# Long-convolution taps of a Macaron layer: products over 64 x 16 positions in place of 128 x 8

## The chip, the cores and the metric

The kernel runs on one core of a Trainium2 chip. The metric is the device time of one execution in microseconds (us). A core has TensorE (PE in the profile; PEld is its weight load), VectorE (DVE), ScalarE (ACT), GpSimd (POOL) and SyncE (SP, which here only issues DMAs).[...]

## The reference

A Macaron layer over x (4 sequences of 1024 positions, 256 channels): half a feed-forward layer, a long convolution along the sequence, half a feed-forward layer again, each on a layer norm and added to x. Cut to what matters:

```python
x = x + 0.5 * ffn(layernorm(x))
x = x + attn(layernorm(x))
x = x + 0.5 * ffn(layernorm(x))

# ffn: 256 -> 1024 (two, gated) -> 1024 -> 1024 -> 256
h = silu(tlin(x, w1)) * tlin(x, w2)
h = gelu(tlin(h, h1)); h = gelu(tlin(h, h2))
return tlin(h, w3)

# attn: a diagonal state-space convolution, its kernel K has 1024 taps per channel
dt = exp(log_dt)[:, None]; A = -exp(log_A_real) + 1j * A_imag
C = (C_real + 1j * C_imag) * (exp(A * dt) - 1) / A
K = 2 * einsum('dn,dnl->dl', C, exp((A * dt)[:, :, None] * t)).real   # 32 modes n
y = irfft(rfft(K, 2 * L) * rfft(x, 2 * L))[:L]
return gelu(y) @ W.T + b
```

Everything is float32.

## The kernel before

**Blocks.** The 4096 positions are cut into 8 blocks of 512. The first feed-forward layer runs over blocks f0 to f7, the second over g0 to g7, one after the other, in `ffn` (L247). In a block, the first layer makes `pa` and `pb` (L254, L255), the second and third make `p` (L268), each in 8 columns m of 16 matmuls (`linear`, L239: 8 input tiles, each as a high and a low part), and the output product `po` (L295) ends it. A column is evicted by ScalarE (activation into `g`, copy into `h`, L271 and L273) and VectorE (low part, L217). The next block's input is loaded, normalised and transposed (`pt`, L225) by `prepare` (L774), which advances one step (`ahead`) per column of the third layer.

**Side work.** All that is not feed-forward is one Python generator, `all_aside` (L794): first the taps of the convolution (`kernel_steps`, L446), then their spectrum (`kernel_spectrum`, L610, products `pf_k`), then for each sequence b the convolution itself (`mix`, L638: spectrum of x with products `pf_m`, product with the taps' spectrum, inverse transform with sums on VectorE, products `pi` L731, Gelu into `yt`, products `pw` L751), then comparisons of the weights held with those given (L328). `ffn` calls `tick` 15 times a block: after each column but the last of the second and third layers, and once before the output product. Each tick runs the generator to its next `yield`. So the order on every engine is fixed by where the yields stand.

`mix(b)` waits in the generator until block f(2b+1) is done. The blocks g(2b) and g(2b+1) need its result in HBM (x2), so `prepare` for a g block begins with

```python
            while ("m", blk // 2) not in done:
                next(aside, None)
            xb = load_x(x2, blk, f"x_{name}")
```

which runs all missing steps of the side work at once; `done` gets its entry when the generator is resumed after the last `yield` of `mix`.

**The taps.** Position t of a tap is split as t = NB a + b. For each channel a product over 128 rows (32 modes, real and imaginary, for two halves of the channels) gives all positions: the stationary operand holds the powers at NB a (128 values of a), the moving one, `qd`, those at b times C (8 values of b for each half of the channels, the other half's rows zero). Powers at NB a are an outer product of 16 fine and 8 coarse powers (`to_re`, `to_im`): three VectorE operations for 4 channel pairs (L525 to L527). `powers` (L422) makes a 128 x 512 tile of powers with exp and sin on ScalarE. The channel pairs come in two groups of 64. The four products of a step are issued one tick after their operand (`ready`, `products`); when a PSUM tile `pk` is full (32 pairs), ScalarE copies it to the four `taps` tiles (L508).

`taps` has partition a and, for each b, the channels. In `spectrum` (L538) it is multiplied by cosine and sine matrices (`forward`, loaded by `matrix`, L551), and partition p stands for position 8 p + j.

Working tiles of 2 KB a partition (`half`) share 19 buffers[...].

Of the kernel before, what the change touches and what calls it, by code (L numbers as in the profile page):

```python
# [15 lines left out]
ALU = mybir.AluOpType  # L16

P = 128
B, L, D = 4, 1024, 256
HID = 1024  # L20
J = L // P
DC = D // P
KH = HID // P
TB = 512
JT = TB // P
N2 = 32
DD = D // 2
NB = L // P
A0, A1 = 16, 8
JQ = J // 2  # L30
N_CHECKS = 44

# [15 lines left out]
C_A0, C_A1 = 0, A0  # L48
# [43 lines left out]
def macaron_layers(  # L92
# [37 lines left out]
    def half(name, *shape, dtype=F32):  # L130

        return work.tile([P, *(shape or (512,))], dtype, tag="half", name=name, bufs=19)
# [289 lines left out]
    def powers(d0, first, n, name):  # L422


        ch = 512 // n
        at = cst_sb[:, None, first : first + n].to_broadcast([P, ch, n])

        def of(i):
            return adt[:, i, d0 : d0 + ch, None].to_broadcast([P, ch, n])

        a, k, e = (half(f"{t}_{name}", ch, n) for t in ("a", "k", "e"))
        tt(e, of(0), at, ALU.mult)
        nc.scalar.activation(e, e, AF.Exp)
        tt(a, of(1), at, ALU.mult)
        reduce_angle(a, a, k)
        yield
        c = k
        sin_cos(c, a)
        yield
        tt(c, c, e, ALU.mult)  # L440
        tt(a, a, e, ALU.mult)
        yield c, a
# [2 lines left out]

    def kernel_steps():  # L446

        yield from kernel_factors()
        taps.extend(half(f"taps_{i}", 2, 2, DD) for i in range(NB // 2))
        n = TB // P  # L450
        group = 512 // NB
        shape = [P, n, A1, A0]
        for g0 in range(0, DD, group):

            for got in powers(g0, C_A1, A1, f"1_{g0}"):
                yield
            c, i = got
            to_re, to_im = half(f"to_re_{g0}", group, A1), half(f"to_im_{g0}", group, A1)
            ts(to_re, c, column(C_RE), None, ALU.mult)
            stt(to_re, i, column(C_IM), to_re, ALU.mult, ALU.add)  # L460
            ts(to_im, c, column(C_IM), None, ALU.mult)
            stt(to_im, i, column(C_MINUS_RE), to_im, ALU.mult, ALU.add)
            yield
            fine = []
            for d0 in range(g0, g0 + group, 512 // A0):
                for got in powers(d0, C_A0, A0, f"0_{d0}"):
                    yield
                fine.append(got)

            for got in powers(g0, C_B, NB, f"b_{g0}"):  # L470
                yield
            c, i = got
            for t, m in ((c, 0), (i, 1)):
                tt(t, t, c_dt[:, m, g0 : g0 + group, None].to_broadcast([P, group, NB]), ALU.mult)
            yield
            qd = []
            for d1 in range(0, group, per_tile):
                t = half(f"qd_{g0 + d1}", per_tile, 2, NB)
                nc.gpsimd.memset(t, 0.0)
                qd.append(t)  # L480
                for h in range(2):
                    part, ch = slice(h * 64, (h + 1) * 64), slice(d1, d1 + per_tile)
                    tt(t[part, :, h, :], c[part, ch], i[part, ch], ALU.add)
            yield

            pk = None
            ready = []

            def products():

                nonlocal pk
                for d1, a in ready:
                    at = d1 % per_tile
                    if at == 0:
                        pk = psum.tile([P, per_tile, 2, NB], F32, tag="ps", name=f"pk_{g0 + d1}")
                    for i in range(n):
                        nc.tensor.matmul(  # L497
                            pk[:, at + i, :, :].rearrange("p h b -> p (h b)"),
                            a[:, i].rearrange("p a b -> p (a b)"),
                            qd[d1 // per_tile][:, at + i, :, :].rearrange("p h b -> p (h b)"),  # L500
                            start=True,
                            stop=True,
                        )
                    if at + n == per_tile:
                        first = g0 + d1 + n - per_tile
                        for i, t in enumerate(taps):
                            for h in range(2):
                                nc.scalar.copy(  # L508
                                    t[:, :, h, first : first + per_tile],
                                    pk[:, :, h, 2 * i : 2 * i + 2].rearrange("p d b -> p b d"),  # L510
                                )
                ready.clear()

            for d1 in range(0, group, n):
                re, im = fine[d1 // (512 // A0)]
                at = d1 % (512 // A0)

                def outer(coarse, t):
                    return (
                        coarse[:, d1 : d1 + n, :, None].to_broadcast(shape),  # L520
                        t[:, at : at + n, None, :].to_broadcast(shape),
                    )

                a, o = (half(f"{t}_{g0 + d1}", n, A1, A0) for t in ("p", "po"))
                tt(a, *outer(to_re, re), ALU.mult)  # L525
                tt(o, *outer(to_im, im), ALU.mult)
                tt(a, a, o, ALU.add)  # L527
                products()
                ready.append((d1, a))
                yield  # L530
            products()
            yield

# [1 line left out]
    def swapped(t):  # L535
        return t[:, ::-1, :]

    def spectrum(rows_of, name):  # L538

        def add(a, b, op, tag):
            o = half(f"{tag}_{name}", 2, D)
            tt(o, a, b, op)
            return o

        u, v = {}, {}
        order = (0, 2, 1, 3)
        evicted = {}

        def matrix(q):  # L551
            m = half(f"m_{name}_{q}", 2, 2, P)
            nc.sync.dma_start(m, forward[:, 2 * q : 2 * q + 2])
            return m

        def products(q, m):
            ps = []
            for e in range(2):
                ps.append(psum.tile([P, 2, D], F32, tag="ps", name=f"pf_{name}_{q}_{e}"))
                for part in range(2):  # L560
                    nc.tensor.matmul(  # L561
                        ps[e][:, part, :], m[:, e, part, :], rows_of(q + JQ * e), start=True, stop=True
                    )
            other = half(f"f_{name}_{q}", 2, D)
            nc.scalar.copy(other, ps[1])
            evicted[q] = ps[0], other

        def sums(q):
            p, other = evicted.pop(q)
            u[q] = add(p, other, ALU.add, f"u{q}")  # L570
            v[q] = add(p, other, ALU.subtract, f"v{q}")

        m_next = matrix(order[0])
        yield
        got = {}
        for n, q in enumerate(order):
            m = m_next
            if n + 1 < len(order):
                m_next = matrix(order[n + 1])
            products(q, m)  # L580
            if n:
                sums(order[n - 1])
            if n == 3:
                a0 = add(u[0], u[2], ALU.add, "a0")
                a1 = add(u[0], u[2], ALU.subtract, "a1")
            yield
        sums(order[3])
        b0, b1 = add(u[1], u[3], ALU.add, "b0"), add(u[1], u[3], ALU.subtract, "b1")
        yield
        got[0], got[4] = add(a0, b0, ALU.add, "x0"), add(a0, b0, ALU.subtract, "x4")  # L590
        got[2, 6] = add(a1, swapped(b1), ALU.add, "x26")
        got[6, 2] = add(a1, swapped(b1), ALU.subtract, "x62")
        yield
        c, d = add(v[0], swapped(v[2]), ALU.add, "c"), add(v[0], swapped(v[2]), ALU.subtract, "d")
        e, f = add(v[1], swapped(v[3]), ALU.add, "e"), add(v[1], swapped(v[3]), ALU.subtract, "f")
        yield
        g, h = add(e, swapped(f), ALU.add, "g"), add(e, swapped(f), ALU.subtract, "h")
        for key, r, by, t in (
            ((1, 7), g, SQRT_HALF, c),
            ((5, 3), g, -SQRT_HALF, c),  # L600
            ((3, 5), swapped(h), SQRT_HALF, d),
            ((7, 1), swapped(h), -SQRT_HALF, d),
        ):
            got[key] = half(f"x{key[0]}{key[1]}_{name}", 2, D)
            stt(got[key], r, by, t, ALU.mult, ALU.add)
            if key == (5, 3):
                yield
        yield got

    def kernel_spectrum():  # L610
# [2 lines left out]
            return taps[j // 2][:, j % 2].rearrange("p h d -> p (h d)")  # L613

        got = None
        for got in spectrum(rows_of, "k"):
            yield
        minus = half("k_minus", 2, D)
        for n, m in enumerate((0, 4)):
# [292 lines left out]
```

## Time and profile before

| | |
|---|---|
| median of 3 runs | 1465.45 us (1464.86 to 1466.04) |
| the profiled execution | 1466.05 us, its span 1464.1 us |
| granted TensorE clock | 0.995 |
| PE busy | 1429.7 us, 98% |
| PEld busy | 1213.7 us, 83% |
| DVE busy | 860.5 us, 59% |
| ACT busy | 666.1 us, 45% |
| POOL busy | 74.4 us, 5% |
| tap products `pk` on PE | 256 records, first at 156.8, last at 437.7 us |
| copies `taps` <- `pk` on ACT | 32, 237 ns median |

The span is the time from the first to the last instruction of the profiled execution, about 2 us less than its device time. Busy times overlap. Every float32 matmul of the tap products leaves two records, each with its own weight load. A row of a group reads: line, engine, operation, output <- inputs (for a matmul the moving operand comes first), shapes, count, then busy time, mean ns of one, idle time of the engine just before it and what ended that. In the strip of 40 slices each digit is the busy share of 36.6 us in tenths. A line of waits reads: who waited, for whom, us in total, times, longest. A line of the chain or the timeline reads: start, us, engine, what.

### The profile page before, as it was taken

How to read it: one execution, taken by the hardware profiler on the slowest of the kernel's cores; microseconds unless marked ns; L12 is line 12 of the kernel's file. 1: busy time of each engine (PE TensorE's matmuls, PEld its weight loads, DVE VectorE, ACT ScalarE, POOL GpSimd, SP SyncE). 2: the span in 40 equal slices, each digit the busy share in tenths (PEclk: the TensorE clock that was granted, in tenths of full speed). 3: DMA queues.
4: the chain of work that ended last, by engine and by line, in shares of the span. 5: the costliest groups of instructions: out<-in, count | busy, mean ns of one | idle time of the engine just before them, and what ended most of it. 6: DMA issues, size and time to landing. Idle time of an engine off the chain costs nothing.

```text
span 1464.1 us, 18076 instructions
## 1 busy us (share of the span) xinstructions
PE 1429.7 (98%) x7074; PEld 1213.7 (83%) x7074; DVE 860.5 (59%) x1616; ACT 666.1 (45%) x996; POOL 74.4 (5%) x71
## 2 busy tenths in 40 slices
PE   5999999999999999997999999999999999999997
PEld 4788888888888888886888888888888888888886
DVE  5776574765744634667367673676736667464521
ACT  3677353783534434442454344543445334353432
POOL 2000000000000000000100001000010000100000
PEclk9999999999999999999999999999999999999999
DMA  9110000100001111210312113121121111633000
GB/s 365 33 42 2 15 30 4 40 1 29 15 29 44 62 46 38 72 58 29 101 51 87 37 36 94 48 89 37 36 94 44 65 37 36 221 117 101 21 9 17
DMA packets 42975, 85.50 MB, mean 58 GB/s; under 512 B 4737, under 2 KB 9985, under 8 KB 42881
## 3 DMA queue, kind: packets, MB, share of 16 engines
q1 hardware_dynamic: 39088, 72.73, 15.1%
q0 software_dynamic: 3792, 11.54, 2.2%
q8 instruction: 57, 0.93, 0.3%
q14 instruction: 38, 0.30, 0.1%
HBM read 69.05 MB, written 15.20 MB: 58 GB/s over the span
## 4 chain that ended last, share of the span: by engine, by line
PE 94%; DMA 2%; DVE 2%; ACT 1%; issue 0%; POOL 0%; SPq 0%; POOLq 0%; DVEq 0%
PE p_f L239 32%; PE p_g L239 30%; PE po_f L295 4%; PE po_g L295 4%; PE pa_g L239 4%; PE pb_g L239 4%; PE pa_f L239 3%; PE pb_f L239 3%; PE pi L731 2%; PE pf_m L561 2%; PE pk L497 2%; PE pw L751 2%; DMA x_f<-in_x_dram 1%; DMA k_in<-in_kin_dram 1%; PE pt_f L225 1%; DVE given L328 1%
## 5 line engine op out<-in xcount | busy, mean ns | idle before, releaser
L239 PE MATMUL p_f<-ha_f,h_sb 128*128 128x512 f32 x1024 | 242.4, 394 | 1.8 <-ACT ha_f L261 0.9
L239 PE MATMUL p_f<-h_f,h_sb 128*128 128x512 f32 x1024 | 240.4, 392 | 0.0
L239 PE MATMUL p_g<-h_g,h_sb 128*128 128x512 f32 x1024 | 236.0, 390 | 0.0
L239 PE MATMUL p_g<-ha_g,h_sb 128*128 128x512 f32 x1024 | 234.5, 390 | 0.0
L239 PEld LDWEIGHTS p_f<-ha_f,h_sb 128*128 128x128 f32 x1024 | 192.2, 189 | 43.5 <-ACT ha_f L261 1.6
L239 PEld LDWEIGHTS p_g<-ha_g,h_sb 128*128 128x128 f32 x1024 | 192.2, 188 | 39.9
L239 PEld LDWEIGHTS p_g<-h_g,h_sb 128*128 128x128 f32 x1024 | 192.2, 188 | 39.8
L239 PEld LDWEIGHTS p_f<-h_f,h_sb 128*128 128x128 f32 x1024 | 190.9, 188 | 40.0 <-DVE h_f L217 0.3
L271 ACT ACTIVATE g_g<-p_g,sc_sb 128x512 f32<-128x512 f32 x128 | 88.2, 689 | 273.4 <-PE p_g L239 268.6
L217 DVE TENSOR_TENSOR h_f<-g_f,h_f 128x512 fp32r<-128x512 f32 x128 | 88.3, 691 | 193.0 <-ACT h_f L273 192.8
L271 ACT ACTIVATE g_f<-p_f,sc_sb 128x512 f32<-128x512 f32 x128 | 88.0, 688 | 245.6 <-PE p_f L239 245.3
L217 DVE TENSOR_TENSOR h_g<-g_g,h_g 128x512 fp32r<-128x512 f32 x128 | 88.4, 691 | 171.4 <-ACT h_g L273 171.1
L273 ACT CAST h_g<-g_g 128x512 fp32r<-128x512 f32 x128 | 79.4, 620 | 3.9
L273 ACT CAST h_f<-g_f 128x512 fp32r<-128x512 f32 x128 | 79.1, 619 | 3.4
L258 ACT ACTIVATE g_g<-pa_g,sc_sb 128x512 f32<-128x512 f32 x64 | 44.0, 687 | 66.5 <-PE pa_g L239 64.4
L239 PE MATMUL pa_f<-xt_f,w_sb 128*128 128x512 f32 x256 | 70.5, 395 | 1.8 <-DVE xt_f L229 1.2
L259 DVE SCALAR_TENSOR_TENSOR g_g<-pb_g,sc_sb,g_g 128x512 f32<-128x512 f32 x64 | 47.9, 748 | 37.2 <-PE pb_g L239 29.8
L239 PE MATMUL pb_f<-xt_f,w_sb 128*128 128x512 f32 x256 | 69.2, 392 | 0.0
L239 PE MATMUL pa_g<-xt_g,w_sb 128*128 128x512 f32 x256 | 68.6, 390 | 0.0
L239 PE MATMUL pb_g<-xt_g,w_sb 128*128 128x512 f32 x256 | 68.4, 389 | 0.0
L295 PE MATMUL po_g<-w_sb,h_g 128*128 128x256 f32 x512 | 64.2, 285 | 2.2 <-DVE h_g L217 2.2
L295 PEld LDWEIGHTS po_g<-w_sb,h_g 128*128 128x128 f32 x512 | 62.3, 192 | 2.9 <-DVE h_g L217 2.8
(216 smaller groups left out, 1682.3 us busy)
## 6 DMA issues: line engine op xcount, KB each, us to landing
h_sb<-in_h_dram POOLq DMA_DIRECT2D x8, 1024.0 KB, 22.6
given<-in_h_dram SPq DMA_DIRECT2D x32, 256.0 KB, 4.7
kr<-k_hat SPq DMA_DIRECT2D x20, 256.0 KB, 2.7
ki<-k_hat SPq DMA_DIRECT2D x20, 256.0 KB, 2.9
x_f<-in_x_dram SPq DMA_DIRECT2D x8, 512.0 KB, 3.8
xr_f<-in_x_dram SPq DMA_DIRECT2D x16, 256.0 KB, 3.5
x<-y_f SPq DMA_DIRECT2D x16, 256.0 KB, 2.4
xm<-x SPq DMA_DIRECT2D x8, 512.0 KB, 4.1
```

Of the source, the lines that this page charges most:

```text
L217: tt(t[:, 1, :], src, t[:, 0, :].bitcast(F32), ALU.subtract)
L225: nc.tensor.transpose(pt[:, i * P : (i + 1) * P], xn[:, i, k * P : (k + 1) * P], ident)
L239: nc.tensor.matmul(ps, w[:, k, m * P : (m + 1) * P], acts[k][:, part, :], start=(k == 0 and part == 0), stop=(k == n - 1 and part == parts ...
L258: nc.scalar.activation(g, pa, AF.Silu, scale=sc_sb[:, 0, m : m + 1])
L259: stt(g if split else t[:, 0, :], pb, sc_sb[:, 1, m : m + 1], g, ALU.mult, ALU.mult)
L271: nc.scalar.activation(g, ps, AF.Gelu, scale=sc_sb[:, layer, m : m + 1])
L273: nc.scalar.copy(t[:, 0, :], g)
L295: nc.tensor.matmul(ps[:, e * D : (e + 1) * D], ha[k][:, part, (i + e) * P : (i + e + 1) * P], w3_sb[:, k, :], start=(k == 0 and part == 0) ...
L497: nc.tensor.matmul(pk[:, at + i, :, :].rearrange("p h b -> p (h b)"), a[:, i].rearrange("p a b -> p (a b)"), qd[d1 // per_tile][:, at + i, ...
L561: nc.tensor.matmul(ps[e][:, part, :], m[:, e, part, :], rows_of(q + JQ * e), start=True, stop=True)
L731: nc.tensor.matmul(banks[dc][e][:, q * P : (q + 1) * P], vs[q + JQ * e][:, part, dc * P : (dc + 1) * P], m[:, e, part, :], start=(part == ...
L751: nc.tensor.matmul(ps[:, e * D : (e + 1) * D], yts[dc][j // JQ][:, (j % JQ + e) * P : (j % JQ + e + 1) * P], wt_sb[:, dc, :], start=(dc == 0),
```

## The change

The split becomes t = 16 a + b, with 64 values of a (8 coarse by 8 fine) and 16 of b. A product's stationary operand has 64 columns and its moving one 32. An outer-product step covers 8 channel pairs instead of 4, so there are 16 steps instead of 32. The `b` powers of a group come in two chunks of 32 channel pairs instead of one call for 64, and the fine powers in one call instead of two. A `pk` tile holds 16 pairs, uses partitions 0 to 63, and is copied twice into each `taps` tile: b from 0 to 7 to partitions 0 to 63, b from 8 to 15 to partitions 64 to 127. So partition 64 o + a stands for row 2 a + o of before, and for the taps `matrix` loads the rows of `forward` in that order, in two DMAs.

```diff
--- before.py
+++ after.py
@@ -25,8 +25,9 @@
 JT = TB // P
 N2 = 32
 DD = D // 2
-NB = L // P
-A0, A1 = 16, 8
+
+NA, NB = 64, 16
+A0, A1 = 8, 8
 JQ = J // 2
 N_CHECKS = 44
 
@@ -445,10 +446,11 @@
 
     def kernel_steps():
 
+
         yield from kernel_factors()
-        taps.extend(half(f"taps_{i}", 2, 2, DD) for i in range(NB // 2))
-        n = TB // P
-        group = 512 // NB
+        taps.extend(half(f"taps_{i}", 2, 2, DD) for i in range(J // 2))
+        n = 512 // NA
+        group = 512 // A1
         shape = [P, n, A1, A0]
         for g0 in range(0, DD, group):
 
@@ -461,27 +463,26 @@
             ts(to_im, c, column(C_IM), None, ALU.mult)
             stt(to_im, i, column(C_MINUS_RE), to_im, ALU.mult, ALU.add)
             yield
-            fine = []
-            for d0 in range(g0, g0 + group, 512 // A0):
-                for got in powers(d0, C_A0, A0, f"0_{d0}"):
+            for fine in powers(g0, C_A0, A0, f"0_{g0}"):
+                yield
+
+            qd = []
+            some = 512 // NB
+            for d0 in range(g0, g0 + group, some):
+                for got in powers(d0, C_B, NB, f"b_{d0}"):
                     yield
-                fine.append(got)
-
-            for got in powers(g0, C_B, NB, f"b_{g0}"):
+                c, i = got
+                for t, m in ((c, 0), (i, 1)):
+                    by = c_dt[:, m, d0 : d0 + some, None].to_broadcast([P, some, NB])
+                    tt(t, t, by, ALU.mult)
+                for d1 in range(0, some, per_tile):
+                    t = half(f"qd_{d0 + d1}", per_tile, 2, NB)
+                    nc.gpsimd.memset(t, 0.0)
+                    qd.append(t)
+                    for h in range(2):
+                        part, ch = slice(h * 64, (h + 1) * 64), slice(d1, d1 + per_tile)
+                        tt(t[part, :, h, :], c[part, ch], i[part, ch], ALU.add)
                 yield
-            c, i = got
-            for t, m in ((c, 0), (i, 1)):
-                tt(t, t, c_dt[:, m, g0 : g0 + group, None].to_broadcast([P, group, NB]), ALU.mult)
-            yield
-            qd = []
-            for d1 in range(0, group, per_tile):
-                t = half(f"qd_{g0 + d1}", per_tile, 2, NB)
-                nc.gpsimd.memset(t, 0.0)
-                qd.append(t)
-                for h in range(2):
-                    part, ch = slice(h * 64, (h + 1) * 64), slice(d1, d1 + per_tile)
-                    tt(t[part, :, h, :], c[part, ch], i[part, ch], ALU.add)
-            yield
 
             pk = None
             ready = []
@@ -495,7 +496,7 @@
                         pk = psum.tile([P, per_tile, 2, NB], F32, tag="ps", name=f"pk_{g0 + d1}")
                     for i in range(n):
                         nc.tensor.matmul(
-                            pk[:, at + i, :, :].rearrange("p h b -> p (h b)"),
+                            pk[0:NA, at + i, :, :].rearrange("p h b -> p (h b)"),
                             a[:, i].rearrange("p a b -> p (a b)"),
                             qd[d1 // per_tile][:, at + i, :, :].rearrange("p h b -> p (h b)"),
                             start=True,
@@ -504,21 +505,21 @@
                     if at + n == per_tile:
                         first = g0 + d1 + n - per_tile
                         for i, t in enumerate(taps):
-                            for h in range(2):
+                            for over in range(NB // J):
+                                b0 = over * J + 2 * i
                                 nc.scalar.copy(
-                                    t[:, :, h, first : first + per_tile],
-                                    pk[:, :, h, 2 * i : 2 * i + 2].rearrange("p d b -> p b d"),
+                                    t[over * NA : (over + 1) * NA, :, :, first : first + per_tile],
+                                    pk[0:NA, :, :, b0 : b0 + 2].rearrange("p d h b -> p b h d"),
                                 )
                 ready.clear()
 
             for d1 in range(0, group, n):
-                re, im = fine[d1 // (512 // A0)]
-                at = d1 % (512 // A0)
+                re, im = fine
 
                 def outer(coarse, t):
                     return (
                         coarse[:, d1 : d1 + n, :, None].to_broadcast(shape),
-                        t[:, at : at + n, None, :].to_broadcast(shape),
+                        t[:, d1 : d1 + n, None, :].to_broadcast(shape),
                     )
 
                 a, o = (half(f"{t}_{g0 + d1}", n, A1, A0) for t in ("p", "po"))
@@ -535,7 +536,8 @@
     def swapped(t):
         return t[:, ::-1, :]
 
-    def spectrum(rows_of, name):
+    def spectrum(rows_of, name, over=1):
+
 
 
 
@@ -550,7 +552,11 @@
 
         def matrix(q):
             m = half(f"m_{name}_{q}", 2, 2, P)
-            nc.sync.dma_start(m, forward[:, 2 * q : 2 * q + 2])
+            for o in range(over):
+                nc.sync.dma_start(
+                    m[o * (P // over) : (o + 1) * (P // over)],
+                    forward.rearrange("(a o) j t k -> o a j t k", o=over)[o, :, 2 * q : 2 * q + 2],
+                )
             return m
 
         def products(q, m):
@@ -613,7 +619,7 @@
             return taps[j // 2][:, j % 2].rearrange("p h d -> p (h d)")
 
         got = None
-        for got in spectrum(rows_of, "k"):
+        for got in spectrum(rows_of, "k", over=NB // J):
             yield
         minus = half("k_minus", 2, D)
         for n, m in enumerate((0, 4)):
```

## The prediction

> **What bounds the kernel now.** I read the page first: busy shares, slices, chain by engine.
>
> ```profile
> PE 1429.7 (98%) x7074; PEld 1213.7 (83%) x7074; DVE 860.5 (59%) x1616; ACT 666.1 (45%) x996; POOL 74.4 (5%) x71
> PE   5999999999999999997999999999999999999997
> PE 94%; DMA 2%; DVE 2%; ACT 1%; issue 0%; POOL 0%; SPq 0%; POOLq 0%; DVEq 0%
> ```
>
> TensorE is the bound: 94% of the chain is PE. VectorE and ScalarE have slack, so the VectorE work that the change removes pays nothing by itself. What can pay is (a) time PE spends on the convolution-kernel products, and (b) the one dip inside the run, the "7" in slice 19 (695 to 732 us). The start (slice 0) is loading and is not touched.
>
> For (a), the groups with shapes kept apart, then PE's timeline at 161 us:
>
> ```profile
> L497 PEld LDWEIGHTS pk<-qd,p 128*128 128x128 f32 x256 | 33.3, 191 | 2.3
> L497 PE MATMUL pk<-qd,p 128*128 128x16 f32 x256 | 30.7, 252 | 0.0
> ```
> ```profile
> 161.34 0.96 PE L497 MATMUL pk<-qd,p 128*128 128x16 f32 x8
> 162.14 3.93 PE L239 MATMUL p_f<-h_f,h_sb 128*128 128x512 f32 x16
> 165.91 0.96 PE L497 MATMUL pk<-qd,p 128*128 128x16 f32 x8
> ```
>
> Each of the 128 products leaves two records, hence x256. The column after the operation is the stationary shape, here 128 rows by 128 columns, and the moving tile has 16 columns. A feed-forward column of 16 matmuls takes 3.63 us alone (chain: "480.94 3.63 PE p_f"). With four products behind it the period is 165.91 - 161.34 = 4.57, and over the next ones 4.58. So a step of four costs 0.95 us of PE, 32 steps 30.4 us. The blocks confirm it: from output product to output product f1 takes 186.08 - 98.44 = 87.64; a block without side work takes 80.23 (last block) + 0.79 for its transposes; the rest is 6.6 = seven steps.
>
> For (b), the chain of waits on PE, then the chain that ended last at two places:
>
> ```profile
> PE pt_f L225 <- DVE x_f L211: 13.8, 1, 13.8
> PE pi L731 <- DVE v_False L722: 7.4, 1, 7.4
> PE po_g L295 <- DVE h_g L217: 2.2, 2, 1.3
> ```
> ```profile
> 629.88 7.68 PE po_f L295 x64
> 692.11 9.49 PE pi L731 x64
> 740.03 7.67 PE po_f L295 x64
> 822.88 7.67 PE po_g L295 x64
> 877.73 7.14 PE pi L731 x64
> 923.27 7.67 PE po_g L295 x64
> ```
>
> Apart from the first transposes, PE has one long wait: 7.4 us, once, for VectorE's inverse-transform sums, and those `pi` products then run 9.49 instead of 7.14. Block f7 (629.88 to 740.03) is 110.15 long; block g1, with the same side work (`pi`, `pw`, three `pf_m`), is 100.39. The difference, 9.8, is the stall.
>
> Why only there: each block gives 15 ticks, and preparing g0 needs mixing 0 finished. Its demand, counted in the generators: factors 6, two groups of 32, spectrum 15, mixing 35, one resume: 121. Seven blocks plus the seven ticks of f7's second layer offer 112. The loop in `prepare` forces the missing nine at once, and they contain VectorE's whole tail of mixing 0. Before g2, g4 and g6 five are missing; those begin at `pi`, whose inputs are ready, and PE does not wait.
>
> **What the Trainium skill says.** "TensorE: Matmul & The Clock Gate", section "LDWEIGHTS (loading the stationary operand)": load time goes with the stationary columns, at columns / 1.2 ns, so 107 for 128 and 53 for 64, and not with rows. The trace agrees: `pi`, also 128 columns, spends 7.14 us on 64 records, 112 ns each, and `pk` 0.95/8 = 119 with entry. Better still, the trace has one load with a single column:
>
> ```profile
> L835 PEld LDWEIGHTS p_bad<-ones,total x2: 79/80/82, 1456.4 to 1456.4; 128*1 128x1 f32 x2
> ```
>
> 191 - 80 = 111 ns for 127 columns, 0.87 ns each. The same page, section "Wait — 56ns, not 53.3ns?", gives a floor of about 25 ns from matmul start to start; no row shows a case that meets it. "TensorEngine Tiling (Array Packing)", "Key Properties": changing the tiling mode drains the engine. The trace does not show a return from such a change; `p_bad` has nothing after it.
>
> **The change part by part.**
>
> 1. *Products* (L497). Still 128, so 256 records, but 64 stationary columns and 32 moving ones. Loads set the pace before (two records move 2 x 16 columns in almost nothing), so a record falls from 112 to 64 x 0.87 = 56 ns. Moving 32 columns instead of 16 stays under that (`pi` streams 128 in 112 ns, so 32 in about 28). A step of eight has 16 x 56 = 0.90 us plus an entry of 0.95 - 8 x 0.112 = 0.05: 0.95, and there are 16. New PE time 15.2; I take 15.9 for uneven pacing. **Gain 14.5.** Bounds: 45 ns a record gives 12.3 (gain 18); columns not mattering gives 16 x (16 x 0.112 + 0.05) = 29.5 (gain 0.9). A drain of up to 0.17 us on entry and on exit (from the one-column matmul's 163 ns) would take 32 x 0.17 = 5.4 back.
>
> 2. *Ticks.* A group now yields 4 (coarse) + 3 (fine) + 8 (two `b` chunks) + 9 (outer loop) = 24 times instead of 32: 16 fewer. Demand before g0 falls to 105 of 112 offered: nothing is forced, `pi` of mixing 0 lands in f6's third layer at tick pace. Before g2, 140 of 142: none. Before g4, 175 of 172: three, only `pw`. Before g6, 210 of 205: five, as before, and from there both kernels are in the same place, the weight checks too. **Gain 9.7** (7.37 waiting + 2.35 slow `pi`). Next to be late: in f6 the next block's norm shares VectorE with the sums: 0.7 + 1.7 + 4 x 0.6 = 4.8 us, ready 6.1 after PE's third column, where PE wants them at 3.63 + 2 x 1.78 = 7.2. A margin of about 1 us.
>
> 3. *VectorE*: outer products 96 to 48 (48 x 0.69 = 33 us less); `c_dt` products 4 to 8 (+2.7); `qd` sums 8 to 16 (+3.3); the eight calls of `powers` keep number and size. Net 27 less, behind PE's 98%: nothing.
>
> 4. *ScalarE*: tap copies 32 to 64, half as many partitions, same 64 elements. Eight start within 1.1 us (213.96 to 215.5 with a cast between); every other tick gets such a burst beside 1.3 us of activation and cast, in at least 3.63. Zero; if the move to upper partitions doubled a copy, 2.2 + 1.3 still fits.
>
> 5. *POOL*: memsets of 0.53 us, 4 to 8. POOL is 5% busy. Behind them stand the output additions, which no PE work awaits soon. *SP*: the four `m_k` loads become eight of half size; landing is 3.0 us, the load is issued a tick (3.6) ahead, and a second issue adds 0.33. Behind on SP are the next loads, with blocks of slack. Zero; bounded by 4 x 0.3 if PE waited each time.
>
> 6. *Unseen small waits*: other helpers now fall beside block ends, where PE's last columns leave about half a microsecond of slack. I take 0.7 lost; bounds -1 (one of today's small waits goes) to +3.
>
> Sum: -14.5 - 9.7 + 0.7 = -23.5. The profiled execution (1466.05, span 1464.1) becomes 1442.5, span 1440.6; it lay 0.6 above the median of 1465.45, so the median forecast is **1442.0**.
>
> **Rivals.**
> - *Columns do not set the pace* (the array is filled at full width, or the change of form drains each time so that little remains): products gain 0.9 only, 1465.45 - 10.6 + 0.7 = 1455.5. For it: no load of 64 columns in the trace. Against: the 80 ns load. 0.12.
> - *The stall moves*: the same sums are waited for in f6, or a block end pays; 9.7 comes back in part, say 8: 1450. For: the 1 us margin. Against: five-step forcings cost nothing today. 0.10.
> - *The change of form keeps loads from running ahead*: each record then pays load and matmul in turn, 136 + 163 = about 300 ns, 256 of them 77 us for 30.4; less the 9.7, 1502. It decides against the change from (30.4 + 9.7)/256 = 157 ns a record. For: the drain sentence. Against: both `p_bad` loads start at 1456.4, the second not held by the first matmul. 0.04.
> - *The schedule does not follow the count*, so that the nine forced steps stay: 1451.7. The counted positions match the trace for all blocks before. 0.02.
>
> **How the numbers follow.** The forecast case has the remaining 0.72: 1438.5 (45 ns) to 1447.5 (drains). The range of 8 in 10 runs from 1438.0 to 1452.0: it takes in the moved stall and leaves out the first rival and the slow one. About 0.2% (3 us) is what a measurement here can tell from no change. Only the drain rival is slower; between drain and no drain a record of some 150 ns would give "same".
>
> **What would show it.** Right: `pk` loads near 135 ns (80 + 64 x 0.87), 16 bursts of about 0.95 us, PE without a wait at `pi`, f7 near 100 us instead of 110, VectorE about 27 us less, the last two g blocks unchanged. Wrong: bursts of 1.8 us or more, gaps on PE before or after them, or a PE wait for `v_False` or `h_f` in f6.

## The result and the profile after

The changed kernel takes 1446.8 us (median of 4, 1445.27 to 1448.97) against 1465.65 before (4 runs): a ratio of 0.9874, with a 95% interval of [0.9859, 0.9889], some 18.5 us less. The forecast was 1442.0 with a range of 1438.0 to 1452.0. The profiled execution took 1447.1, its span 1445.3, 18.8 less than the span before.

The page of the changed kernel, busy shares, PE's slices and the chain by engine (the lines of the file have moved by one to six):

```profile
PE 1418.6 (98%) x7074; PEld 1199.6 (83%) x7074; DVE 835.7 (58%) x1580; ACT 672.7 (47%) x1026; POOL 76.1 (5%) x75
PE   5999999999999999999999999999999999999997
PE 93%; DMA 3%; DVE 3%; ACT 1%; issue 0%; POOL 0%; SPq 0%; POOLq 0%; DVEq 0%
```

The "7" in slice 19 is gone and nothing has come in its place. PE is the bound as before. VectorE lost 24.8 us of work; none of PE's waits had been for that work, so by itself this bought nothing.

The waits of PE, longest first, and then the chain from the output product of f5 to that of f6:

```profile
PE pt_f L226 <- DVE x_f L212: 13.6, 1, 13.6
PE po_g L296 <- DVE h_g L218: 1.7, 2, 1.3
```
```profile
538.22 7.67 PE po_f L296 x64
...
607.57 7.14 PE pi L737 x64
...
629.96 3.46 PE pw L757 x16
633.42 7.67 PE po_f L296 x64
```

`pi` of mixing 0 now lies in f6 (from the output product of f5 to that of f6), runs its undisturbed 7.14 us, and PE no longer waits for `v_False`. By PE's timeline, f7 lasts 88.2 us instead of 110.0; f6 has taken over `pi` and `pw` and lasts 95.1 instead of 88.3.

The products themselves, by the tile `pk` and then in the chain. The records of one tick that stand together are called a burst here; a burst and the feed-forward column after it make a step:

```profile
L498 PEld LDWEIGHTS pk<-qd,p x256: 132/138/138, 156.8 to 342.6; 128*64 128x64 f32 x128
```
```profile
161.77 1.05 PE pk L498 x16
162.82 3.85 PE p_f L240 x16
166.67 1.05 PE pk L498 x16
```

A load has 138 ns where the forecast said 135. But a step takes 166.67 - 161.77 = 4.90 us. Less the column alone (3.63) that is 1.27, where the forecast had 0.95: the burst is 1.05 instead of 0.90, and the column after it is 0.22 longer, not 0.05. Sixteen steps cost 20.3 us instead of the 15.2 worked out and the 15.9 taken.

So the account of the span is: products 30.4 to 20.3, -10.1; stall of f7, -9.75 (f7 less g1 in the profile before); about +1 in block g6 (84.8 against 83.8 us). Sum -18.8, as measured. Nothing ties the last term to the change: in the kernels below, with the same work in g6, that block takes anything from 83.2 to 85.4.

One thing has to be known to read the times below: the moment at which f0's output product starts lies between 95.4 and 98.7 us in these profiles, although the tap products begin only after it. Part of that is the granted clock: between 40 and 50 us it was 0.83 to 0.85 in five of the twelve profiles, where that moment is at 97.2 or later, and 1.00 in the other seven, where it is at 97.0 or earlier. Before and after are both among the five. Steps inside a profile are therefore compared, rather than single times. The five kernels below for which no time is given were executed once each (1436.6 to 1453.3 us); only their steps are read.

### The profile page after: what moved, and what is told of

It is laid out like the page before. It is cut to its first block, busy times and chain, and to the rows that moved or that the text cites. A ratio compares the mean times of both kernels' runs of the same rounds, so it can differ in the third digit from the quotient of the medians.

```text
span 1445.3 us, 18115 instructions
## 1 busy us (share of the span) xinstructions
PE 1418.6 (98%) x7074; PEld 1199.6 (83%) x7074; DVE 835.7 (58%) x1580; ACT 672.7 (47%) x1026; POOL 76.1 (5%) x75
## 4 chain that ended last, share of the span: by engine, by line
PE 93%; DMA 3%; DVE 3%; ACT 1%; issue 0%; POOL 0%; SPq 0%; POOLq 0%; DVEq 0%
PE p_f L240 31%; PE p_g L240 30%; PE po_g L296 4%; PE po_f L296 4%; PE pa_g L240 4%; PE pb_g L240 4%; PE pa_f L240 4%; PE pb_f L240 4%; PE pi L737 2%; PE pf_m L567 2%; PE pw L757 2%; PE pk L498 1%; DMA x_f<-in_x_dram 1%; DMA k_in<-in_kin_dram 1%; DMA x_g<-x 1%; PE pt_f L226 1%
## 5 line engine op out<-in xcount | busy, mean ns | idle before, releaser
L272 ACT ACTIVATE g_g<-p_g,sc_sb 128x512 f32<-128x512 f32 x128 | 88.3, 690 | 273.7 <-PE p_g L240 273.6
L218 DVE TENSOR_TENSOR h_f<-g_f,h_f 128x512 fp32r<-128x512 f32 x128 | 88.2, 691 | 202.9 <-ACT h_f L274 202.6
```

The lines of the kernel that those rows point to most:

```text
L218: tt(t[:, 1, :], src, t[:, 0, :].bitcast(F32), ALU.subtract)
L272: nc.scalar.activation(g, ps, AF.Gelu, scale=sc_sb[:, layer, m : m + 1])
```

## The experiments

**Schedule alone.** Theory: half of the gain is the tick count and has nothing to do with 64 by 16. Rival: the stall only moves, or the new form of the products is what counts. The first kernel is that of before, with two outer-product steps to a tick:

```diff
-            for d1 in range(0, group, n):
-                re, im = fine[d1 // (512 // A0)]
+            for d2 in range(0, group, 2 * n):
+                fresh = []
+                for d1 in (d2, d2 + n):
+                    re, im = fine[d1 // (512 // A0)]
...
-                products()
-                ready.append((d1, a))
+                    fresh.append((d1, a))
+                products()
+                ready.extend(fresh)
                 yield
```

> The kernel before with its 128 by 8 products, but two outer-product steps to a tick, so that the side work has the 16 ticks fewer of the change and nothing else of it. Schedule theory: the wait of pi in f7 goes, f7 falls from 110.0 to about 88 us and f6 takes the pi and pw products; products cost 30.4 less 16 exits of 0.15, so the time falls by 9.7 + 2.4 = 12, to about 1453.5. Rival, the stall only moves to f6: the time stays within 3 us of before.

Measured: 1454.85 us, ratio 0.9934 [0.9917, 0.9950], which is 9.7 us, give or take 2.4. PE's waits, longest first:

```profile
PE pt_f L225 <- DVE x_f L211: 14.1, 1, 14.1
PE po_g L295 <- DVE h_g L217: 1.8, 2, 1.3
```

No `pi`; f7 lasts 88.2 us. The time alone could hold the 2.4 us expected on top, but the timeline has no room for them: the two bursts of a tick mostly stand apart, with some 6 or 7 matmuls of the feed-forward column between them, and there are 30 bursts, where the kernel before has 32. The kernel's text issues these two bursts one right after the other. So the yields do not fix the order on PE down to the single matmul, as the description of the kernel before has it; what moved them apart, no run shows.

The second kernel is the changed one with the tick count of before:

```diff
                 ready.append((d1, a))
                 yield
+                yield
```

> The changed kernel with one empty yield more after each of the 16 outer-product steps, so that the tick count of the kernel before is back and the 64 by 16 products stay. Schedule theory: nine steps are forced before g0 again, PE waits 7.4 us for v_False, the time rises by 9.7 to about 1456.5. Rival, the changed form of the products itself brought the time: it stays near 1446.8.

Measured: 1454.34 us, ratio 0.9938 [0.9921, 0.9954]: 0.0064 above the change, or 9.4 us of its gain undone. Each kernel is set against the kernel before as timed beside it. The wait is back, word for word apart from the line numbers:

```profile
PE pi L738 <- DVE v_False L729: 7.4, 1, 7.4
```

The two parts add up: 0.9934 x 0.9938 = 0.9872, against 0.9874 for the change. The tick count brings about 9.7 us and the products about 9.1, each within some 2.4. The stall did not move.

**What a record costs.** A burst is longer than forecast. Three theories: the moving columns add to the load (sum), the load sets the pace (load), or the change between 128 and 64 columns costs something (form). The first kernel loads 128 columns again, with 32 moving:

```diff
-                            pk[0:NA, at + i, :, :].rearrange("p h b -> p (h b)"),
-                            a[:, i].rearrange("p a b -> p (a b)"),
+                            pk[:, at + i, :, :].rearrange("p h b -> p (h b)"),
+                            a[:, i // 2 * 2 : i // 2 * 2 + 2].rearrange("p d a b -> p (d a b)"),
...
```

> The changed kernel, each product with the operand of two channel pairs as 128 stationary columns, 32 moving ones as in the change; the result for a pair is read from the half of the partitions that is its own (128 copies instead of 64). Sum theory, a record costs its load and its moving columns one after the other[...], a burst of sixteen 1.9 us, a step 2.1. Load theory, the load alone sets the pace and moving is hidden: 100 to 112 ns, burst 1.6 to 1.8. Form theory, the 0.22 us on the column after a burst is the change between 64 and 128 columns: here it falls to 0.15 as before.

Its chain:

```profile
160.75 1.71 PE pk L498 x16
162.46 3.75 PE p_f L240 x16
```

The burst takes 1.71, where the sum theory wanted 1.9: 107 ns a record, so 32 moving columns are hidden behind a load of 128. The column after the burst is 0.12 longer, not 0.22, as the form theory said. The whole step takes 1.71 + 3.75 = 5.46, so the products cost 5.46 - 3.63 = 1.83.

The second kernel keeps 64 columns and streams 64:

```diff
-                            pk[0:NA, at + i, :, :].rearrange("p h b -> p (h b)"),
+                            pk[0:NA, at + i // 2 * 2 : at + i // 2 * 2 + 2, :, :].rearrange("p d h b -> p (d h b)"),
...
-                            qd[d1 // per_tile][:, at + i, :, :].rearrange("p h b -> p (h b)"),
+                            qd[d1 // per_tile][:, at + i // 2 * 2 : at + i // 2 * 2 + 2, :, :].rearrange("p d h b -> p (d h b)"),
```

> The changed kernel with 64 stationary columns and 64 moving ones in each product: the columns of the neighbouring pair are streamed too and overwrite its result, so half the taps are wrong ones. Sum theory: [...]burst 1.28 us, step 1.5. Load theory: moving stays hidden, 66 ns, burst 1.05, step 1.27 as in the change. The burst against that of the change (1.05) tells them apart.

```profile
164.01 1.08 PE pk L498 x16
165.09 3.85 PE p_f L240 x16
```

1.08 instead of 1.05, where the sum theory wanted 1.28: it falls. Up to 64 moving columns are nearly free here.

**Slope and offset.** What remains is either a load that is slower than its columns say, or a cost for each burst. Issuing the products of two steps together halves the number of bursts:

```diff
                 tt(a, a, o, ALU.add)
-                products()
+                if d1 // n % 2 == 0:
+                    products()
```

> The changed kernel with the products of two outer-product steps issued in one tick: 8 bursts of 32 records instead of 16 of 16. Burst theory: 66 ns a record and 0.22 us for each burst, so a burst with its end takes 2.32 and all of them 18.6 instead of 20.3 us, time down by 1.8. Record theory, the 0.22 goes with the records: 2.54 a burst, no gain.

```profile
158.10 1.98 PE pk L498 x32
160.08 7.48 PE p_f L240 x32
```

Two columns alone are 7.26 us. So thirty-two records and what follows cost 9.46 - 7.26 = 2.20 us, sixteen cost 1.27. Two points give a line: (2.20 - 1.27)/16 = **58 ns a record and 0.34 us a burst**. The single records agree: inside a burst they start 58 ns apart (median). The 2.20 is better than the 2.32 expected, since 66 ns a record had the entry of a burst in it. The eight bursts cost 17.6 instead of 20.3, and the kernel takes 1443.26 us, ratio 0.9860 [0.9841, 0.9878]: below the change, with an interval that overlaps its. Inside the profiles, from f0's output product to that of g7, this kernel is 2.6 us shorter than the changed one, as the steps say.

The same for 32 columns, in bursts of 16 and 32:

```diff
-                            pk[0:NA, at + i, :, :].rearrange("p h b -> p (h b)"),
-                            a[:, i].rearrange("p a b -> p (a b)"),
+                            pk[0:32, at + i, :, :].rearrange("p h b -> p (h b)"),
+                            a[:, i].rearrange("p a b -> p (a b)")[:, 0:32],
...
```

> The changed kernel with only the first 32 of the 64 stationary columns in each product; the other half of the taps stays zero. Column theory, a record's pace follows its columns: 107 ns at 128 and 66 at 64 go on to about 45 at 32, burst 0.7 us. Floor theory, a record cannot go below some 60 to 66 ns however few columns it loads: burst stays at 1.0 to 1.05 us.

> The changed kernel with the first 32 stationary columns only (the other half of the taps stays zero) and the products of two steps in one tick. With 32 columns a burst of 16 and its end cost 0.84 us. Column theory, 28 ns a record and the rest for each burst: 32 records 1.29 us. Floor theory, a record stands on its own at 50 ns: 32 records 1.66.

Chain with bursts of 16, then with bursts of 32:

```profile
160.11 0.62 PE pk L500 x16
160.73 3.85 PE p_f L240 x16
```
```profile
159.37 1.13 PE pk L500 x32
160.50 7.48 PE p_f L240 x32
167.97 1.13 PE pk L500 x32
```

0.84 and 8.60 - 7.26 = 1.34 us: 31 ns a record and again 0.34 a burst. The floor theory falls.

**Which loads pay for a burst.** At full width the line through 8 records (0.95, before, with 16 moving columns) and 16 (1.83, with 32) is 110 ns and 0.07 us. So the narrow products pay 0.27 more for each burst. Is it the form, or any load below full width? 96 columns tell:

```diff
-                            pk[0:NA, at + i, :, :].rearrange("p h b -> p (h b)"),
-                            a[:, i].rearrange("p a b -> p (a b)"),
+                            pk[0:96, at + i, :, :].rearrange("p h b -> p (h b)"),
+                            a[:, i // 2 * 2 : i // 2 * 2 + 2].rearrange("p d a b -> p (d a b)")[:, 0:96],
```

> The changed kernel with 96 stationary columns (64 of a pair and 32 of its neighbour) and 32 moving ones; half the taps are made from the wrong pair. From 16 and 32 records a burst, 64 columns cost 58 ns a record and 0.34 us a burst; full width 111 ns and 0.06. Form theory, the 0.34 belongs to products that leave half of the array's columns out: 96 columns run in the full form, 16 x 84 ns + 0.06 = 1.40 us with the column after. Width theory, every load below 128 columns pays it: 16 x 84 ns + 0.34 = 1.68.

```profile
161.04 1.30 PE pk L498 x16
162.34 3.76 PE p_f L240 x16
```

5.06 - 3.63 = 1.43. There is only one length of burst here, so no line gives the offset; but inside a burst the records start 85 ns apart (median), which leaves 1.43 - 16 x 0.085 = 0.07. 96 columns pay as full width does, 32 and 64 columns pay the 0.34. That is what the form theory says.

The timeline shows where the offset lies. A load and the matmul after it, at the head of a burst with 96 columns, then with 64:

```profile
160.65 1.58 PEld L498 LDWEIGHTS pk<-qd,p 128*96 128x96 f32 x16
160.88 1.47 PE L498 MATMUL pk<-qd,p 128*96 128x32 f32 x16
```
```profile
161.70 1.01 PEld L498 LDWEIGHTS pk<-qd,p 128*64 128x64 f32 x16 [0.35 <-issue]
161.70 1.12 PE L498 MATMUL pk<-qd,p 128*64 128x32 f32 x16
```

With 96 columns the first load starts 0.23 us ahead of its matmul, while the wide matmul before it still runs. With 64 columns the weight loads pause for 0.35 us, and the first load starts only with its matmul; the same holds for the first wide load after the burst. From the last wide matmul to the first narrow one pass 0.32 us (medians of the records' starts), with 96 columns 0.23; from the last narrow one to the first wide one 0.15 pass, which is 0.09 more than the distance inside the burst, with 96 columns nothing more. So of the 0.27, 0.09 lies at each end, and most of the rest at the second record of the burst, which with 96 columns follows the first after 28 ns because its load was not behind. Inside the burst loads run ahead in both forms.

**A version from this.** Full width avoids the offset, half as many products avoid loads: two channel pairs in one product, of which the two diagonal blocks are used.

```diff
-                    for i in range(n):
+                    for i in range(0, n, 2):
...
-                            pk[0:NA, at + i, :, :].rearrange("p h b -> p (h b)"),
-                            a[:, i].rearrange("p a b -> p (a b)"),
-                            qd[d1 // per_tile][:, at + i, :, :].rearrange("p h b -> p (h b)"),
+                            pk[:, at + i : at + i + 2, :, :].rearrange("p d h b -> p (d h b)"),
+                            a[:, i : i + 2].rearrange("p d a b -> p (d a b)"),
+                            qd[d1 // per_tile][:, at + i : at + i + 2, :, :].rearrange("p d h b -> p (d h b)"),
...
-                                nc.scalar.copy(
-                                    t[over * NA : (over + 1) * NA, :, :, first : first + per_tile],
-                                    pk[0:NA, :, :, b0 : b0 + 2].rearrange("p d h b -> p b h d"),
-                                )
+                                for odd in range(2):
+                                    nc.scalar.copy(
+                                        t[over * NA : (over + 1) * NA, :, :, first + odd : first + per_tile : 2],
+                                        pk[odd * NA : (odd + 1) * NA, odd::2, :, b0 : b0 + 2].rearrange("p d h b -> p b h d"),
+                                    )
```

> The changed kernel with two channel pairs in one product: 128 stationary columns (64 positions of each pair), 64 moving ones, 64 products instead of 128; each pair is read from its own half of the partitions, with 128 copies of 32 elements instead of 64 of 64. Load theory: 8 records of 107 ns a step and the end of before, 0.95 us, sixteen times 15.2 instead of 20.3; time down by 5 to about 1441.7. Rival, the moving columns or the copies count: ScalarE has 1.8 us more in every other tick; then PE waits for a PSUM bank and the gain stays under 2.

Chain and copies:

```profile
159.51 0.84 PE pk L498 x8
160.35 3.73 PE p_f L240 x16
```
```profile
L511 ACT COPY taps<-pk x128: 178/183/188, 160.4 to 339.2; 64x32 f32<-64x32 f32 x128
```

4.57 - 3.63 = 0.94 a step, 15.0 us in all. 1440.32 us (1439.3 to 1441.72), ratio 0.9838 [0.9823, 0.9853]: its interval lies below that of the change, and the two ratios are about 5.3 us apart. That is not the luck of the start: from f0's output product to that of g7 its profile is 5.7 us shorter than that of the change (1325.7 against 1331.4). PE has no new wait; the 128 copies stay hidden.

The same with the products of two steps in one tick:

> The same two-pair products, two steps in one tick: 8 bursts of 16 records. By the full-width measurement (1.71 and 0.12 us) 8 x 1.83 = 14.6 instead of 20.3; time down by 5.7 from the change, 0.6 below the two-pair kernel. Rival, the merged burst makes the column after it late: no better than the two-pair kernel.

```profile
167.51 1.73 PE pk L498 x16
169.24 7.36 PE p_f L240 x32
```

9.09 - 7.26 = 1.83 a burst, 14.6 in all as expected, and 1440.28 us, ratio 0.9835 [0.9819, 0.9852]. The steps of the two kernels differ by 0.4 us, where 0.6 was expected; in the times that is below what these runs can tell. Their two lengths of burst give the line of full width at one and the same form, 64 moving columns: (1.83 - 0.94)/8 = 111 ns a record and 0.05 us a burst, close to the 110 and 0.07 above.

## Why the prediction was right, and by how much not

- **What bounds.** Right: PE before and after, and the removed VectorE work (27 forecast, 24.8 measured) paid only through the ticks.
- **Ticks and stall.** Right in mechanism and size: 9.7 forecast, 9.7 and 9.4 in the kernels that move the ticks alone; in the profile of the second of these f7 is 9.3 longer than g1. The margin in f6 held, `pi` did not wait. The sign "f7 near 100 us instead of 110" was wrong, and against the forecast's own count, which put `pi` into f6: with `pi` and `pw` gone too, f7 takes 88.2.
- **Load by columns.** Right: 0.87 ns a column from the one-column load; measured 58 ns a record at 64 (56 forecast) and 31 at 32. "TensorE: Matmul & The Clock Gate" of the Trainium skill, section "LDWEIGHTS (loading the stationary operand)", with columns / 1.2 ns (53 and 27), agrees to some 5 ns. Moving columns hidden: right. The prediction found no row near the least distance between starts that it cites; the trace has one, the two one-column matmuls of `p_bad`, which start 26 ns apart.
- **Zeros.** ScalarE's copies, POOL's memsets and SP's split loads cost nothing on PE: none appears among PE's waits. The 0.7 us for small waits was a guess; nothing ties the profile's +1 in g6 to it.
- **Rivals.** That columns do not set the pace falls by the slope. The moved stall falls by the kernel with the ticks alone, and the schedule that does not follow the count by `pi` in f6. That loads no longer run ahead falls as it was priced, for each record: 256 records at 300 ns were 77 us, and they take 20.3. At the two ends of each burst it is what happens.

**The step that failed** is the burst's term, "plus an entry of 0.95 - 8 x 0.112 = 0.05". It was carried over from 128-column products standing among 128-column products. Among them 64-column ones pay 0.34: 16 x 0.29 = 4.6 us, and with 58 instead of 56 ns a record that makes the 5.1 between 20.3 and 15.2. The 0.7 added "for uneven pacing" hid part of it, so that the products miss by 4.4 of the 4.7 us that the whole sum is off; that allowance was not worked out from anything, and its help is luck. The forecast had a price for the offset, up to 5.4 us of drains, but only in the bounds.

The profile before had shown a part of this offset, a third of the 0.27 by which narrow bursts exceed wide ones. These are its last wide loads and the one-column product:

```profile
1455.63 0.67 PEld L295 LDWEIGHTS po_g<-w_sb,h_g 128*128 128x128 f32 x5
1456.43 0.09 PEld L835 LDWEIGHTS p_bad<-ones,total 128*1 128x1 f32 x2
1456.43 0.19 PE L835 MATMUL p_bad<-ones,total 128*1 128x1 f32 x2
```

The wide loads end at 1456.30; the load of `p_bad`, whose operand `total` had been there since 1363.8, starts at 1456.43, together with its matmul. That matmul starts 209 ns after the one before it, where the `po_g` ones stand 120 apart: the same 0.09 on the way in. The prediction read in these rows only that the second load is not held by the first matmul. With no matmul after it and two records, `p_bad` could not show the way out.

The page "TensorEngine Tiling (Array Packing)" of the Trainium skill, section "Key Properties", says that changing the tiling mode drains the engine; a cost that 32 and 64 columns pay and 96 and 128 do not, and loads that stop running ahead at both ends of the burst, fit that. That it is this drain is argued from the pattern; no run shows the mode itself.

## What to carry to other kernels

When side work is issued by ticks, count the ticks against each deadline: removing steps from a generator can be worth as much as the engine time they cost, and one empty `yield` more or less tests it. For float32 products with as few moving columns as here (16 to 64), PE's price was the stationary columns loaded, so try to share a load among results before making it narrower: two pairs to a full load took 15.0 us, one pair to half a load 20.3. Narrow products between wide ones should come in long bursts, since here each burst paid 0.34 us.

## What was not expected of the hardware

- 32- and 64-column products between 128-column ones cost 0.34 us a burst, with records of 31 and 58 ns; 96 and 128 columns cost 0.05 to 0.07, with 85 and 110 ns.
- At the head of a 32- or 64-column burst the first load starts with its matmul, 0.35 us after the load before it ended; at 96 and 128 columns it starts 0.23 us ahead of its matmul.
- Copying from PSUM partitions 0 to 63 to SBUF partitions 64 to 127 is no slower than staying: all 64 copies of the changed kernel, half of which move, take 204 to 208 ns.
